# Sums of K through DRAM, a head's product in half the array, and a later transpose of scales in a linear-attention kernel with an FP4 FFN

## The chip, the cores and the metric

One Trainium2 chip, one NeuronCore. The metric is the device time of one execution in microseconds (us). TensorE is called PE here, its weight loads PEld, VectorE DVE, ScalarE ACT, GpSimd POOL and SyncE SP.

## The reference, cut to what matters

The input is 4 batches of 2048 rows of 256 floats. All arithmetic is in fp32.

```python
xn = layernorm(x)
q, k, v = xn @ Wq + bq, xn @ Wk + bk, xn @ Wv + bv      # 16 heads of 64
Q, K = elu(q) + 1, elu(k) + 1
KV = einsum('bshd,bshm->bhdm', K, v)                    # per head 64 x 64
Z  = 1 / (einsum('bshd,bhd->bsh', Q, K.sum(axis=1)) + 1e-6)
o  = einsum('bshd,bhdm,bsh->bshm', Q, KV, Z)
x1 = layernorm(xn + o @ Wo + bo) * g1 + be1
s  = layernorm(x1 + gelu(x1 @ W1 + b1) @ W2 + b2) * g2 + be2
# the gate: inputs and weights of each linear are quantized to FP4 in blocks of 16
h  = silu(fp4_linear(xn, w_gate)) * fp4_linear(xn, w_up)
out = x + s * silu(fp4_linear(h, w_down))
```

## The kernel before

The rows are cut into 32 blocks of 256 (8 per batch, two row tiles of 128 each); block n is worked on in turn n of the main loop. All of a batch's K must be known before its first block, so turn n also computes a part of the next batch's keys: a `sub` is one block of rows with one half (512 columns, 8 heads) of Wk, and two subs go into each turn (16 per batch). Blocks 24 to 31 belong to the last batch and have no subs (`subs` is empty). The first batch's keys and the FP4 quantizing of the weights are done ahead of the loop, in the opening.

**Keys.** V is never formed. Per sub, `keys_k` makes K (tiles pk, k1, e, kk) and adds it to `kacc` on POOL; `keys_xk` adds K^T xn into two PSUM banks, pxk. When a half is complete, `m_of_half` turns it into `m` = (K^T V) Wo. It is a generator and is stepped in three pieces:

1. `pxk` is copied out to `xk` (ACT). `pks`, four products with a column of ones, gives K's sums with the features on the partitions; DVE puts them into `kh`, from which the denominators are made. `pkb`, one product of a matrix of ones with kacc, gives the same sums in a row, the same on all partitions; ACT copies it to `ksum`.
2. `pkv` is K^T xn Wv for four pairs of heads, each as a full 128 x 128 product over two chunks of 128, of which only the two 64 x 64 blocks on the diagonal are used. Eight DVE instructions (L465) add bv times ksum and write these blocks into `kv`, which is zero elsewhere.
3. `pm`, kv times Wo, copied to m.

In the loop the first piece runs at the end of the turns n with n mod 8 = 3 or 7 (n = 3, 7, 11, 15, 19, 23), the other two in the next turn. The first batch's first half is done in the opening, its second half across the opening's end and turn 0.

**The FP4 side.** The products of the gate, pg (gate and up) and pd (down), need their quantized inputs transposed. The grid values (bf16, tile `grid`) are transposed by a DMA into `gridT` (`grid_T`, L549). The block scales (tile `scale`) are small; `spread_scales` transposes them on PE (`pscale`, L533), copies them out on ACT (`scaleT`, L535), stores them to DRAM (`scale_d`, L537), and loads them back with eight DMAs, each of which repeats one row of scales over 16 partitions, into `qT` (L540). `quantized_x` and `quantized_h` then multiply qT by gridT on DVE (L557, L562). In turn n the scales for turn n + 1 are spread: those of h of block n + 1 and of x of block n + 2.

**The order of a turn.** `q_of` (pq, then q1, e, zq), `sums` (pz, the denominators, in four column quarters of the array, then a reciprocal and a broadcast through DRAM), `gate_up` of the next block (pg), `down` (pd), `qz`, `attention` (pa, then the layer norm), the rest of the keys, `ffn_2` of the block before (py), the scales of h and x (L210 to L216), `x1_T` (pt_x, then x1T), `spread_scales`, the last four products of ffn_2, the grid work, `output` of the block before, and `ffn_1` (pf, then hT with Gelu). In a turn without subs, q_of of the next turn follows ffn_1 at once, with pd and pz behind it.

Inside the loop PE keeps the order in which the program writes its instructions (`tc.keep_in_program_order`). The order of the other engines and of the DMA queue on SP comes from a scheduler, which places ready work by its own estimates, so a change in one place can move instructions elsewhere. PSUM has four banks for single products (tag `mm`) and two each for pxk and for running sums (pa, py, pd).

Of the kernel before, what the change touches and what calls it, by code (L numbers as in the profile page):

```python
# [8 lines left out]
F32 = mybir.dt.float32  # L9
BF16 = mybir.dt.bfloat16  # L10
AF = mybir.ActivationFunctionType
ALU = mybir.AluOpType
AX = mybir.AxisListType

P = 128
# [6 lines left out]
def linear_attention_gated_by_fp4_ffn(  # L22
# [34 lines left out]
    nc = tc.nc  # L57
    B, S, D = src.shape
    HD = Wq.shape[1]
    DH = 64  # L60
    FF = W1.shape[1]
    I = w_gate.shape[0]
    ND = D // P
    NH = HD // P
    NF = FF // P
# [12 lines left out]
    work = ctx.enter_context(tc.tile_pool(name="work", bufs=2))  # L78
    small = ctx.enter_context(tc.tile_pool(name="small", bufs=4))
    dram = ctx.enter_context(tc.tile_pool(name="dram", bufs=2 * NB, space=bass.MemoryType.DRAM))  # L80
# [3 lines left out]
    def mm_tile(name):  # L84
        return ps.tile([P, 512], F32, tag="mm", name=name)
# [12 lines left out]
    def mm(*args, **kw):  # L98
        ins = nc.tensor.matmul(*args, **kw)  # L99
        if in_order[0]:  # L100
            tc.keep_in_program_order(ins)
        return ins
# [44 lines left out]
    ones = const.tile([P, P], F32, name="ones")  # L147
# [272 lines left out]
    def m_of_half(b, f, dep=None):  # L420

        nm = f"{b}_{f}"
        fs = slice(f * HALF, (f + 1) * HALF)
        wv = batch.tile([P, ND, HALF], F32, tag="wv", name=f"wv_{nm}", bufs=1)
        load_when(dep, wv, by_chunks(Wv)[:, :, fs])
        wo = batch.tile([P, 4, D], F32, tag="wo", name=f"wo_{nm}", bufs=1)
        load_when(dep, wo, by_chunks(Wo)[:, 4 * f : 4 * f + 4, :])
        if f == 0:
            kh[b] = batch.tile([P, NH, 32], F32, tag="kh", name=f"kh_{b}")
            nc.gpsimd.memset(kh[b], 0.0)  # L430
        m = m_sb[b, f] = batch.tile([P, 4, D], F32, tag="m", name=f"m_{nm}", bufs=3)
        kacc = keys.pop((b, "acc", f))
        pxk = keys.pop((b, "pxk", f))
        xk = batch.tile([P, ND, HALF], F32, tag="xk", name=f"xk_{nm}", bufs=1)
        for d in range(ND):
            nc.scalar.copy(xk[:, d, :], pxk[d])
        pks = mm_tile(f"pks_{nm}")
        for c in range(4):
            mm(
                pks[:, c : c + 1], kacc[:, c * P : (c + 1) * P], ones[:, 0:1],  # L440
                start=True, stop=True,
            )
        for i in range(2):
            hs = slice(i * DH, (i + 1) * DH)
            r0 = 2 * f + i
            nc.vector.tensor_copy(kh[b][hs, 4 * f : 4 * f + 4, r0], pks[hs, :4])
        pkb = mm_tile(f"pkb_{nm}")
        mm(pkb, ones, kacc, start=True, stop=True)
        ksum = work.tile([P, 4, P], F32, tag="e", name=f"ksum_{nm}", bufs=3)
        nc.scalar.copy(ksum, pkb.rearrange("p (c f) -> p c f", c=4))  # L450
        yield
        pkv = mm_tile(f"pkv_{nm}").rearrange("p (c f) -> p c f", c=4)
        kv = work.tile([P, 4, P], F32, tag="kv", name=f"kv_{nm}", bufs=1)
        nc.gpsimd.memset(kv, 0.0)
        for ci in range(4):
            cs = slice(ci * P, (ci + 1) * P)
            for d in range(ND):
                mm(
                    pkv[:, ci, :], wv[:, d, cs], xk[:, d, cs], start=d == 0, stop=d == ND - 1
                )  # L460
        for ci in range(4):
            for h in range(2):
                hs = slice(h * DH, (h + 1) * DH)
                c = 4 * f + ci
                nc.vector.scalar_tensor_tensor(  # L465
                    kv[hs, ci, hs], ksum[hs, ci, hs], cols["bv"][hs, c : c + 1],
                    pkv[hs, ci, hs], ALU.mult, ALU.add,
                )
        yield
        for c2 in range(2):  # L470
            pm = mm_tile(f"pm_{nm}_{c2}").rearrange("p (c d) -> p c d", c=2)
            for ci in range(2):
                mm(
                    pm[:, ci, :], kv[:, 2 * c2 + ci, :], wo[:, 2 * c2 + ci, :],
                    start=True, stop=True,
                )
            nc.scalar.copy(m[:, 2 * c2 : 2 * c2 + 2, :], pm)
        yield
# [221 lines left out]
        nc.gpsimd.tensor_tensor(x1, x1, rows["g1"], ALU.mult)  # L700
        nc.gpsimd.tensor_tensor(x1, x1, rows["shift"], ALU.add)

    def ffn_1(n):
        x1T = blk[n].pop("x1T")
        hT = work.tile([P, NF, T], F32, tag="big", name=f"hT_{n}")
        blk[n]["hT"] = hT
        for cc in range(0, NF, 2):
            pf = mm_tile(f"pf_{n}_{cc}").rearrange("p (c t) -> p c t", c=2)
            for ci in range(2):
                c = cc + ci  # L710
                for d in range(ND):
                    mm(
                        pf[:, ci, :], w1_sb[:, d, c * P : (c + 1) * P], x1T[:, d, :],
                        start=d == 0, stop=d == ND - 1,
                    )
            for ci in range(2):
                c = cc + ci
                nc.scalar.activation(
                    hT[:, c, :], pf[:, ci, :], AF.Gelu, bias=cols["b1"][:, c : c + 1]
                )  # L720

    def ffn_2(n, j, chunks=range(NF)):
        if "py" not in blk[n]:
            blk[n]["py"] = acc_tile(f"py_{n}").rearrange("p (j d) -> p j d", j=TB)
        py, hT = blk[n]["py"], blk[n]["hT"]
        for c in chunks:
            mm(
                py[:, j, :], hT[:, c, j * P : (j + 1) * P], w2_sb[:, c, :],
                start=c == 0, stop=c == NF - 1,
            )  # L730
# [73 lines left out]
    for n in range(NBLK):  # L804
        b, bi = divmod(n, NB)
        subs = (2 * bi, 2 * bi + 1) if b + 1 < B else ()
        if n < last:
            gate = gate_up(n + 1)
        for sub in subs:
            keys_T(b + 1, sub)  # L810
        if subs:
            q_of(n)
            load_xnT(n + 1)
            _, kk_ins = keys_k(b + 1, subs[0])
            with tc.issue_after(kk_ins):
                ins = quantized_x(n)
            with tc.issue_after(sums(n, ins.ins).ins):
                for j in range(TB):
                    quantized_h(n, j)
            step(m_half)  # L820
            keys_xk(b + 1, subs[0])
            step(gate, 9)
            step(m_half)
            down(n, 0)
            down(n, 1)
        elif n < last:
            def values():
                quantized_h(n, 0)
                return quantized_x(n)

            q_of(n, values)
            quantized_h(n, 1)
            load_xnT(n + 1)
            down(n, 0)
            sums(n)
            step(m_half)
            step(gate, 9)
            step(m_half)
            down(n, 1)
        else:  # L840
            for j in range(TB):
                quantized_h(n, j)
                down(n, j)
        with tc.issue_after(blk[n + 1]["late"]) if n < last else nullcontext():
            qz(n)
        if subs:
            keys_k(b + 1, subs[1])
        elif n > 0:
            ffn_2(n - 1, 0, range(NF // 2))
        attention(n)  # L850
        if n + 2 < NBLK:
            load_xn(n + 2)
        if subs:
            keys_xk(b + 1, subs[1])
            if subs[1] % NB == NB - 1:
                m_half = m_of_half(b + 1, subs[1] // NB)
                step(m_half)
        bn, bin_ = divmod(n + 1, NB)
        if bn + 1 < B:
            for sub in (2 * bin_, 2 * bin_ + 1):  # L860
                keys_in(bn + 1, sub)
        if n > 0:
            ffn_2(n - 1, 0, range(0 if subs else NF // 2, NF))
            ffn_2(n - 1, 1, range(NF // 2))
        more = n + 1 < NBLK, n + 2 < NBLK
        if more[0]:
            for j in range(TB):
                scales_h(n + 1, j)
            if more[1]:
                scales_x(n + 2)  # L870
        x1_T(n)
        if more[0]:
            spread_scales(n + 1, *more)
        if n > 0:
            ffn_2(n - 1, 1, range(NF // 2, NF))
        if more[0]:
            grid_of_h(n + 1, 0)
            grid_T(n + 1, 0, NI)
            grid_of_h(n + 1, 1, blk[n]["act"])
            if more[1]:  # L880
                grid_of_x(n + 2, blk[n]["act"])
            grid_T(n + 1, NI, (NCH if more[1] else NI) * TB)
        if n > 0:
            output(n - 1)
        if n + 1 == last:
            q_of(last)
            sums(last)
        ffn_1(n)
    for j in range(TB):
        ffn_2(last, j)  # L890
        output(last, [j])
# [34 lines left out]
```

## Time and profile before

| what | value |
|---|---|
| three runs | 1972.35, 1974.74, 1977.85 us; median 1974.74 |
| profiled execution | 1976.54 us; span of its instructions 1974.8 us |
| mean granted PE clock | 0.996 |
| busy: PE, PEld, DVE, ACT, POOL | 1931.2, 1395.8, 1268.1, 777.1, 536.5 us |
| pkb: products, records | 8, 16; the two start within 0.5 us |
| pkv: products, records, mean ns of one | 64, 128, 275 |
| kv<-ksum,bcol,pkv (DVE, L465) | 64, about 280 ns each |
| ksum copy (ACT, L450) | 8, 588 ns each |
| pscale in the loop and just before | 32, 273 ns each |
| qT<-scale_d, 128 KB each | 248, 5.7 us from issue to landing |
| scale_d<-scaleT, 64 KB | 32, 2.4 us |
| gridT<-grid | 63, 5.4 us |

An fp32 product shows as two records each of weight load (PEld) and matmul (PE). Records overlap, because matmuls are pipelined: the time that a product holds PE is read from the starts, not from its length. A row such as "PE pscale L105 <- DVE scale L215: 9.1, 7, 4.0" says that PE waited for that instruction of DVE 9.1 us in total, 7 times, at most 4.0. "xN" is how many records a row has merged.

### The profile page before, as it was taken

Reading aid. Unit: us, or ns where it says so; the run is one execution under the profiler, and the core shown is the slowest. Engines: PE = TensorE matmul, PEld = TensorE weight load, DVE = VectorE, ACT = ScalarE, POOL = GpSimd, SP = SyncE. Lnnn points to the kernel's source line nnn. Section 1 sums busy time; section 2 is a strip of 40 time slices with the busy share of each in tenths; the row PEclk is TensorE's granted clock in tenths of the full one; section 3 lists DMA queues with packets and bytes.
Section 4 is the critical chain, followed back from the end, with each engine's and each line's share of the span. In section 5 each row is a group of like instructions: output and inputs, shape, how many; then the busy total and the mean of one; then the engine's idle time right before and its main releaser. Section 6 shows DMA issues by size and latency. Waiting matters only on the chain.

```text
span 1974.8 us, 22636 instructions
## 1 busy us (share of the span) xinstructions
PE 1931.2 (98%) x8020; PEld 1395.8 (71%) x8020; DVE 1268.1 (64%) x2319; ACT 777.1 (39%) x1351; POOL 536.5 (27%) x457
## 2 busy tenths in 40 slices
PE   7889999999999999999999999999999999999998
PEld 3445676777776777777777776777766778777777
DVE  7767566656666666666656566665566666677763
ACT  2335433444333444433434423444333443334442
POOL 4332232213233223232223232222232212222221
PEclk9989999999999999999999999999999999999999
DMA  4544433444433544534443534453534434444441
GB/s 148 185 121 87 111 83 92 107 106 80 87 68 82 106 102 91 118 74 108 90 86 61 105 87 85 106 113 65 107 83 81 74 74 81 83 84 80 86 86 41
DMA packets 202104, 183.30 MB, mean 93 GB/s; under 512 B 80236, under 2 KB 161672, under 8 KB 201992
## 3 DMA queue, kind: packets, MB, share of 16 engines
q1 hardware_dynamic: 201576, 181.08, 42.5%
q8 instruction: 63, 1.03, 0.2%
q10 hardware_dynamic: 416, 0.79, 0.1%
q14 instruction: 49, 0.40, 0.1%
HBM read 133.51 MB, written 31.52 MB: 84 GB/s over the span
## 4 chain that ended last, share of the span: by engine, by line
PE 90%; DVE 6%; DMA 2%; ACT 1%; issue 1%; POOL 0%; SPq 0%; POOLq 0%; DVEq 0%; ACTq 0%
PE pg L99 15%; PE pa L99 11%; PE pf L99 11%; PE pq L99 10%; PE pk L99 10%; PE py L99 10%; PE pxk L99 9%; PE pd L99 8%; PE pz L99 2%; DMA gridT<-grid 1%; PE pm L99 1%; PE pt_x L105 1%; PE pkv L99 1%; PE pt_k L105 1%; DVE kk L398 1%
## 5 line engine op out<-in xcount | busy, mean ns | idle before, releaser
L99 PE MATMUL pg<-wgu,qT 128*128 128x352 f32 x1024 | 309.4, 460 | 0.8 <-DVE qT L557 0.8
L99 PEld LDWEIGHTS pg<-wgu,qT 128*128 128x128 f32 x1024 | 193.6, 190 | 118.4 <-issue 12.5
L402 POOL TENSOR_TENSOR kacc<-kacc,kk 128x512 f32<-128x512 f32 x120 | 171.1, 1426 | 337.9 <-DVE kk L398 333.9
L99 PE MATMUL pk<-wk_sb,xnT_k 128*128 128x512 f32 x512 | 238.3, 610 | 4.2 <-ACT xnT_k L371 3.2
L99 PE MATMUL pxk<-kk,xn_k 128*128 128x512 f32 x512 | 233.5, 596 | 1.1 <-DVE kk L398 1.0
L99 PE MATMUL py<-w_sb,hT 128*128 128x256 f32 x1024 | 232.9, 379 | 0.5 <-DVE s L736 0.5
L99 PE MATMUL pf<-x1T,w_sb 128*128 128x256 f32 x1024 | 228.0, 381 | 0.0
L99 PE MATMUL pa<-m,zq 128*128 128x256 f32 x1024 | 227.2, 380 | 0.3 <-ACT g L600 0.3
L99 PE MATMUL pq<-xnT,wq_sb 128*128 128x256 f32 x1024 | 226.3, 379 | 0.0
L99 PEld LDWEIGHTS pa<-m,zq 128*128 128x128 f32 x1024 | 194.0, 190 | 38.7 <-issue 9.8
L99 PEld LDWEIGHTS py<-w_sb,hT 128*128 128x128 f32 x1024 | 192.4, 190 | 35.5 <-issue 11.0
L99 PEld LDWEIGHTS pf<-x1T,w_sb 128*128 128x128 f32 x1024 | 195.6, 191 | 27.3 <-issue 0.4
L99 PEld LDWEIGHTS pq<-xnT,wq_sb 128*128 128x128 f32 x1024 | 193.6, 190 | 25.8
L605 POOL TENSOR_TENSOR o<-g,be_r 128x512 f32<-128x512 f32 x32 | 47.9, 1497 | 504.3 <-ACT g L600 504.3
L99 PEld LDWEIGHTS pk<-wk_sb,xnT_k 128*128 128x128 f32 x512 | 99.7, 197 | 109.3 <-issue 96.3
L637 DVE SCALAR_TENSOR_TENSOR zq<-e,q 128x512 f32<-128x512 f32 x128 | 87.5, 689 | 137.5 <-ACT e L633 137.4
L99 PE MATMUL pd<-wd,qT 128*128 128x256 f32 x768 | 172.2, 379 | 0.1
L693 ACT ACTIVATE x1T<-pt_x,bcol 128x256 f32<-128x256 f32 x64 | 32.8, 563 | 352.7 <-PE pt_x L105 352.7
L99 PEld LDWEIGHTS pxk<-kk,xn_k 128*128 128x128 f32 x512 | 93.4, 190 | 106.8 <-issue 84.2
L99 PEld LDWEIGHTS pd<-wd,qT 128*128 128x128 f32 x768 | 145.8, 190 | 24.1 <-DVE qT L562 0.5
L321 POOL TENSOR_TENSOR rstd<-rstd,neg_half 128x2 f32<-128x2 f32 (+1 forms) x97 | 73.5, 758 | 300.6 <-DVE rstd L320 252.6
L583 ACT ACTIVATE h<-pg 128x352 f32<-128x352 f32 x128 | 59.0, 461 | 212.0 <-PE pg L99 211.9
(129 smaller groups left out, 2453.3 us busy)
## 6 DMA issues: line engine op xcount, KB each, us to landing
zb<-z_d SPq DMA_DIRECT2D x128, 256.0 KB, 6.0
qT<-scale_d SPq DMA_DIRECT2D x248, 128.0 KB, 5.7
x_k<-in_L_attn_src_dram SPq DMA_DIRECT2D x32, 256.0 KB, 2.8
x<-in_L_attn_src_dram SPq DMA_DIRECT2D x32, 256.0 KB, 2.7
xn_d<-xn_k SPq DMA_DIRECT2D x32, 256.0 KB, 2.0
xnT_d<-xnT_k SPq DMA_DIRECT2D x32, 256.0 KB, 5.5
xn<-xn_d SPq DMA_DIRECT2D x32, 256.0 KB, 2.6
xnT<-xnT_d SPq DMA_DIRECT2D x32, 256.0 KB, 2.7
```

The costliest lines, as they stand in the source:

```text
L99: ins = nc.tensor.matmul(*args, **kw)
L105: ins = nc.tensor.transpose(*args, **kw)
L321: nc.gpsimd.tensor_tensor(rstd[:, j0:j1], rstd[:, j0:j1], neg_half[:, j0:j1], ALU.pow)
L398: ins = nc.vector.scalar_tensor_tensor(kk, e, 1.0, k1, ALU.min, ALU.max)
L402: nc.gpsimd.tensor_tensor(kacc, kacc, kk, ALU.add)
L583: nc.scalar.activation(hh, halves[0], AF.Silu)
L605: nc.gpsimd.tensor_tensor(o, g, rows["be2"], ALU.mult)
L637: nc.vector.scalar_tensor_tensor(zq[:, cc : cc + 2, :], e, 1.0, q1, ALU.min, ALU.max)
L693: ins = nc.scalar.activation(x1T[:, c, :], pt[:, c, :], AF.Identity, bias=cols["be1"][:, c : c + 1], scale=cols["g1"][:, c : c + 1],)
```

## The change

It has three parts. First, pkb is dropped: ACT copies the column pks to a small tile `kcol`, SP stores it to DRAM turned round (`k_d`, 4 x 128), and a second DMA loads it into `ksum`, repeated over all partitions. ksum has its own buffer now. Second, pkv is computed per head: sixteen products of 64 columns by 64, the two heads of a pair in the left and right half of the array's columns. Third, `spread_scales` is called later: in turn 0 in the middle of ffn_1, in turns 24 to 30 behind the last four products of ffn_2. In turns 1 to 23 it stays where it was.

```diff
-        pkb = mm_tile(f"pkb_{nm}")
-        mm(pkb, ones, kacc, start=True, stop=True)
-        ksum = work.tile([P, 4, P], F32, tag="e", name=f"ksum_{nm}", bufs=3)
-        nc.scalar.copy(ksum, pkb.rearrange("p (c f) -> p c f", c=4))
+        kcol = small.tile([P, 4], F32, tag="kcol", name=f"kcol_{nm}")
+        nc.scalar.copy(kcol, pks[:, :4])
+        k_d = dram.tile([4, P], F32, tag="k_d", name=f"k_d_{nm}", bufs=2)
+        nc.sync.dma_start(k_d.rearrange("c f -> f c"), kcol)
+        ksum = work.tile([P, 4, P], F32, tag="ksum", name=f"ksum_{nm}", bufs=1)
         yield
-        pkv = mm_tile(f"pkv_{nm}").rearrange("p (c f) -> p c f", c=4)
+        nc.sync.dma_start(
+            ksum, k_d.rearrange("(o c) f -> o c f", o=1).to_broadcast([P, 4, P])
+        )
+        pkv = mm_tile(f"pkv_{nm}")[:, : 4 * DH].rearrange("p (c f) -> p c f", c=4)
...
         for ci in range(4):
-            cs = slice(ci * P, (ci + 1) * P)
             for d in range(ND):
-                mm(
-                    pkv[:, ci, :], wv[:, d, cs], xk[:, d, cs], start=d == 0, stop=d == ND - 1
-                )
+                for h in range(2):
+                    cs = slice(ci * P + h * DH, ci * P + (h + 1) * DH)
+                    mm(
+                        pkv[h * DH : (h + 1) * DH, ci, :], wv[:, d, cs], xk[:, d, cs],
+                        start=d == 0, stop=d == ND - 1,
+                    )
...
-                    pkv[hs, ci, hs], ALU.mult, ALU.add,
+                    pkv[hs, ci, :], ALU.mult, ALU.add,
...
-    def ffn_1(n):
+    def ffn_1(n, half_way=None):
...
         for cc in range(0, NF, 2):
+            if half_way is not None and cc == NF // 2:
+                half_way()
...
         x1_T(n)
-        if more[0]:
+        if subs and n > 0:
             spread_scales(n + 1, *more)
         if n > 0:
             ffn_2(n - 1, 1, range(NF // 2, NF))
+        if more[0] and not subs:
+            spread_scales(n + 1, *more)
...
-        ffn_1(n)
+        ffn_1(n, None if n else lambda: spread_scales(1, True, True))
```

## The prediction

> **What bounds the kernel now.** I read the page first: the slices, then the chain that ended last.
>
> ```profile
> PE   7889999999999999999999999999999999999998
> DVE  7767566656666666666656566665566666677763
> PE 90%; DVE 6%; DMA 2%; ACT 1%; issue 1%; POOL 0%; SPq 0%; POOLq 0%; DVEq 0%; ACTq 0%
> ```
>
> PE (TensorE) is full from the third slice on, 90% of the chain is PE, and DVE has a third of its time free. So a microsecond of PE work taken out of the main loop is a microsecond of time, unless PE then meets a wait that its work had covered; and a wait of PE in the main loop costs its full length. PE's waits, next, are few. One row belongs to the transpose that is moved:
>
> ```profile
> PE pscale L105 <- DVE scale L215: 9.1, 7, 4.0
> ```
>
> By its tile's instructions these are block 0 (4.0 us) and the blocks 24 to 29, which have no keys to compute: three waits of 0.3 us and three of 1.44 us. Block 30 and the blocks with keys have none. Then PE's timeline at a batch boundary (columns: start, length, engine, line, operation):
>
> ```profile
> 1584.69 0.95 PE L99 MATMUL pks<-ones,kacc 128*128 128x1 f32 x8
> 1585.50 1.10 PE L99 MATMUL pkb<-kacc,ones 128*128 128x512 f32 x2
> 1586.44 5.34 PE L99 MATMUL py<-w_sb,hT 128*128 128x256 f32 x24
> ...
> 1610.40 1.45 PE L99 MATMUL pz<-zq,kh 128*32 128x256 f32 x16
> 1611.77 2.05 PE L99 MATMUL pkv<-xk,wv 128*128 128x128 f32 x16
> 1613.66 9.63 PE L99 MATMUL pg<-wgu,qT 128*128 128x352 f32 x32
> ```
>
> Read it by starts, since lengths overlap: pkb holds PE from 1585.50 to 1586.44, 0.94 us; pkv from 1611.77 to 1613.66, 1.89 us (a product is two records, 0.112 us apart in pkv). Nothing waits between them.
>
> **What the skill says.** (1) The Trainium skill, "TensorEngine Tiling (Array Packing)", Key Properties: column tiles work independently, and a change of tiling mode drains the array. The trace agrees: pz already uses quarters (128*32), and in short windows of its timeline four records start together at 1610.40, the next four at 1610.64, then 1610.85, so four products of 256 columns take about 0.215 us, one product's time; from pz's last group, started at 1611.46, to pkv is 0.31 us, so the change of mode costs about 0.1 us beyond the 0.21 us of work. (2) "TensorE: Matmul & The Clock Gate", Part 1: an idle window of some 3.4 us halves PE's clock. The trace agrees at block 0:
>
> ```profile
> 221.00:226.00 5.00, 0.78 (x4) 0.45 (x4) 4.48 (x11) 1.70 (x3) 3.35 (x4) 1.00 0.03 10
> 226.00:230.00 4.00, 3.96 (x12) 3.18 (x13) 3.14 (x6) 2.18 (x4) 1.55 (x2) 0.58 0.73 241
> ```
>
> The first figure is the stretch, then each engine's busy time; PEclk is third from the end. After 4 us of idle PE the clock is 0.58, and the FFN's first product there (pf, 32 records) takes 8.6 us from start to the next tile instead of 6.9. (3) The same page, on queue depths: ScalarE and VectorE are strict first-in, first-out. The tail below rests on it. (4) "DMA: Bandwidth & Descriptors", Rules for kernel authors: a strided last dimension is one descriptor per element. The new k_d store, 128 partitions by 4 floats turned round, is 512 elements of 4 bytes; no DMA of before is like it.
>
> **The change, part by part, on PE's path.**
>
> *Row sums through DRAM.* pkb goes: 0.94 us at each of the six boundaries inside the loop (blocks 3, 7, 11, 15, 19, 23), **5.6 us**. ACT gets a 128x4 copy for one of 588 ns; that is off the path. SP gets two issues per half, which in the built order stand, in the loop, right before the scale store or the loads of the next keys; the second waits for the first to land. Behind it queue the scale store and its eight broadcasts. In block 23 the copy can be done near 1586, the scale store is due at about 1592.5 (1593.5 now, less 0.94), so the landing may take some 5 us before SP delays it; scale_d lands in 2.4 us and xn_d in 2.0 us, and 512 small elements I put at 3 (2 to 8). The broadcast of 256 KB is like xn_d's loads, 2.6 us, and DVE needs it only 20 us later. Cost taken: 0, to 1 us above.
>
> *K^T xn Wv in halves.* 8 products of 128x128 become 16 of 64x64. If two run together as four do in pz, and loads hide there as in pz, 32 records are 16 pairs of about 0.056 us (half of pkv's 0.112): 0.9 us. Entering costs a weight load less than now; leaving for pg adds a mode change and an exposed load, 0.1 + 0.1. So 1.2 us for 1.89: 0.7 each, six in the loop, **4.3 us**. Bounds: 0.9 each with no switch cost; if the halves run one after the other, 32 x 0.056 + 0.2 = 2.0, a loss of 0.1.
>
> *First batch, f=1 (before and in block 0).* PE would reach pg 1.6 us sooner, but pg waits for DVE's qx (0.84 us now), and that for the gridT transpose; the eight kv instructions (2.3 us) move behind it. I take **0.6**, 0 to 1.6.
>
> *First batch, f=0 (the opening, near 88 to 110 us).* PE waits for DVE's weight quantizing there (2.3 us at 91.87, 1.7 at 108.18), so savings go into these waits. New: ksum's load stands on SP behind five row loads (last issue 99.86) and lands near 103.5 to 104 where DVE wants it at 102.5; behind it wait wgu and wd on DVE; k_d also holds up a wgu load by 1 us. **-0.5**, +1 to -3.
>
> *Block 0's transpose in the middle of ffn_1.* pf can start when x1T is there (ACT, 222.09 + 1.02), so PE works from 222.7 through half of pf to 226.2; the scale (DVE, done 225.9) is ready. But on ACT the second hT now stands behind m_x, which waits for y (228.9), so pf's last chunk finds its PSUM buffer only at 230.0 and pf ends at 231.7, against 234.8 now (which has the wait and the slow clock). **3.0 us**, 1 to 5. The broadcasts start some 4 us later; here qx is 22 us away, so they stay hidden.
>
> *Blocks 24 to 29: transpose behind four products of ffn_2.* PE fills its wait: 3 x 0.3 + 3 x 1.44 = 5.2 us. But look at what follows it (ACT, then DVE, block 25):
>
> ```profile
> 1685.37 1.02 ACT L693 ACTIVATE x1T<-pt_x,bcol 128x256 f32<-128x256 f32 x2 [12.37 <-PE pt_x L105]
> 1687.14 0.27 ACT L535 COPY scaleT<-pscale 128x128 f32<-128x128 f32 x1 [0.74 <-PE pscale L105]
> 1687.30 0.80 ACT L235 ACTIVATE m_h<-h 128x704 bf16<-128x704 f32 x1
> 1688.67 0.63 ACT L235 ACTIVATE m_x<-y 128x512 bf16<-128x512 f32 x1 [0.57 <-DVE y L231]
> ...
> 1701.26 0.96 DVE L562 TENSOR_TENSOR qT<-qT,gridT 128x768 f32<-128x768 f32 x1 [4.81 <-DMA qT<-scale_d]
> ```
>
> The built order puts scaleT behind m_x on ACT, and m_x waits for DVE's y. So scaleT starts near 1689.2 instead of 1687.14, 2.05 us later (1.56 in the blocks with the short wait). With it go scale_d, eight broadcasts and, on SP behind them, gridT; DVE already waits for them (4.81 us), multiplies, and only then makes the zq that pz needs. Measured from pscale, in the three blocks where qx starts late (15.36, 15.49, 15.93) pg starts 4.57 after it; the other three (13.8 to 14.1) have pg at its floor, 19.39. Adding the shift: typical blocks get 15.3 + 4.6 = 19.9 (short wait) or 16.0 + 4.6 = 20.6 (long); two in six have a slow store, 1.6 more, as now. Sum 3 x 19.9 + 3 x 20.55 + 3.2 = 124.6 against 118.7 now: **-5.9 us** net, since both are in DVE's time, which the change leaves; the 5.2 are given back within each block. Bounds: +5 if all hides, -12 if stores are slow in all.
>
> *Block 30.* No wait to win; its eight broadcasts now stand behind gridT on SP, some 3.5 us later; its products are due 3.8 us after they are made. 0.
>
> Sum: 5.6 + 4.3 + 0.6 - 0.5 + 3.0 - 5.9 = 7.1 us. The profiled execution took 1976.54 (span 1974.8), inside the range of the three runs; taken off the median, 1974.74: **1967.6 us**.
>
> **Rivals.**
> 1. *The scale chain is hidden in the tail after all*: the 5.2 us stay won in place of 5.9 lost, 18.2 in all: 1956.5. For: the six blocks wait for nothing but the scale at pscale. Against: the 4.81 us above. Chance 0.15.
> 2. *The change doesn't do what it says: halves run one after the other.* Then pkv costs 2.0 and 4.9 us go: 1972.5. Against: pz's four together. Chance 0.17.
> 3. *Slower: the late scales in the tail.* The same mechanism in full: if the store of the scales is slow in every block (3.0 us to the first broadcast in block 25, 1.6 in block 24) and the waits for pd grow to 3.5 us, so that the clock halves as in block 0. It decides from a tail loss of 13.0 + 5.9 = 19 us, 3.2 a block. At 3.5 a block: 21 us lost, 1982.7. Chance 0.12.
>
> The forecast has 0.52, the rest 0.04.
>
> **From cases to numbers.** 0.3%, 5.9 us, is about what a measurement of this kernel can tell from no change. The forecast's own range is 1963 to 1973, some six tenths of it beyond 5.9 us. With rival 1, faster is 0.53; with rival 2 and the forecast's weak end, same 0.33; slower 0.14. The range reaches down to rival 1 and up past rival 2 to its bounds, and leaves out rival 3 and a part of the rest: 1956.5 to 1977.5.
>
> **What would show it.** Right: pkb gone and pks followed by py at once; pkv near 1.2 us in pairs; PEclk 1.0 at block 0; PE's wait for DVE scale gone; scaleT behind m_x in blocks 24 to 29, and new waits of PE at pd or pz on qT. Wrong: pg still 19.4 us after the scale is ready; pkv at 2 us; SP's k_d landing over 5 us; PE waits in the opening grown by more than 3 us.

## The result, and the profile after

| | before | after |
|---|---|---|
| median of 4 runs each | 1974.83 us | 1984.32 us |
| lowest to highest | 1972.35 to 1977.85 | 1982.2 to 1986.56 |
| profiled execution; span | 1976.54; 1974.8 | 1982.2; 1980.3 |

The ratio is 1.0048, 95% interval 1.003 to 1.0065: the change makes the kernel 9.5 us **slower**. The forecast was 1967.6, with a range up to 1977.5: it is wrong, and on the other side. The profiled execution of after is the lowest of its four runs and that of before lies 1.7 us above its median, so the profiles show 5.5 us of the 9.5.

The page of after, its slices and its chain:

```profile
PE   7878999999999999999999999999999989999998
PE 83%; DVE 7%; DMA 6%; issue 1%; SPq 1%; ACT 1%; POOL 1%; DVEq 0%; POOLq 0%; ACTq 0%
```

PE's work has shrunk (1921.8 us busy, 1931.2 before), yet its share of the chain falls from 90% to 83%, while DMA goes from 2% to 6%. Three slices are a digit lower: the third (the opening), the fourth, which ends with block 0's wait, and the thirty-third, from 1584 us on, where the last batch's boundary (block 23) is. The waits of PE name them (waiting tile, releaser: total, times, longest):

```profile
PE pd L99 <- DVE qT L570: 9.8, 7, 5.8
PE pg L99 <- DVE qT L565: 7.2, 1, 7.2
PE pxk L99 <- DVE kk L398: 5.1, 4, 3.7
...
PE pwgu L105 <- issue: 3.0, 1, 3.0
```

The row "pscale <- DVE scale" (9.1 us) is gone as meant. In its place PE waits 7.2 us once for pg, in block 0, and 5.8 once for pd, at block 23; the other six waits at pd, 4.0 together, are in the tail. The 3.7 and 3.0 are in the opening. What they share is in the DMA rows (out<-in, queue, count, size, median from issue to landing) and in SP's waits:

```profile
k_d<-kcol SPq DMA_DIRECT2D x8, 2.0 KB, 10.4
ksum<-k_d SPq DMA_DIRECT2D x8, 256.0 KB, 4.2
```

```profile
SPq L454 <- DMA k_d<-kcol: 51.2, 7, 10.6
```

The store of 2 KB takes 10.4 us to land, over twice the 256 KB load behind it, and SP stands still for it. (The trace has a landing for two of the eight stores, 11.5 us in the opening and 9.3 at block 23. At the other boundaries of the loop ksum's load, which waits for it, is issued 8.7 to 11.6 us after it.) The boundary at block 23, PE's timeline of after:

```profile
1583.37 0.95 PE L99 MATMUL pks<-ones,kacc 128*128 128x1 f32 x8
1584.18 5.43 PE L99 MATMUL py<-w_sb,hT 128*128 128x256 f32 x24
...
1611.54 4.53 PE L99 MATMUL pd<-wd,qT 128*128 128x256 f32 x12 [5.84 <-DVE qT L570]
1616.00 1.07 PE L99 MATMUL pz<-zq,kh 128*32 128x256 f32 x16
1617.01 1.15 PE L99 MATMUL pkv<-xk,wv 128*64 128x64 f32 x32
1618.09 6.18 PE L99 MATMUL pg<-wgu,qT 128*128 128x352 f32 x20
```

pks runs straight into py: pkb is gone. pkv, 32 records in half columns, holds PE from 1617.01 to 1618.09, 1.08 us for the 1.89 of before. But pd ahead of it waited 5.84 us, and then took 4.46 us from its start to pz instead of 2.69 (1607.71 to 1610.40 before). SP's queue in the same stretch, after:

```profile
1584.97 0.37 SPq L451 DMA_DIRECT2D k_d<-kcol  x1
1594.32 0.32 SPq L454 DMA_DIRECT2D ksum<-k_d  x1
1594.73 0.39 SPq L545 DMA_DIRECT2D scale_d<-scaleT  x1
1599.47 3.63 SPq L548 DMA_DIRECT2D qT<-scale_d  x8
```

and before:

```profile
1593.47 0.32 SPq L537 DMA_DIRECT2D scale_d<-scaleT  x1
1595.06 3.63 SPq L540 DMA_DIRECT2D qT<-scale_d  x8
```

Count from pscale (1589.88 after, 1592.06 before). The scale store is issued 4.85 us later instead of 1.41: 3.44 us are SP's wait for k_d. From that store to the first broadcast it takes 4.74 us instead of 1.59: 3.15 more, with SP waiting for nothing but the landing of the scale store. DVE's first multiplication into qT starts 20.65 us after pscale, before 13.91, so it is 6.7 us late; the two delays make 6.6 of it. They are not of one kind: the trace shows the first as a wait for k_d, but when the scale store goes out k_d has landed (1594.30), and the load of ksum, 256 KB, stands 0.41 us ahead of it.

Block 0, two stretches of after (columns: stretch, then busy time of PE, PEld, DVE, ACT, POOL; PEclk third from the end):

```profile
189.00:196.00 7.00, 0.36 (x1) 0.00 (x0) 0.22 (x1) 0.00 (x0) 0.00 (x0) 0.69 1.22 179
196.00:200.00 4.00, 3.48 (x6) 2.19 (x7) 3.97 (x5) 0.46 (x1) 0.00 (x0) 0.50 0.95 271
231.00:238.00 7.00, 5.58 (x25) 4.46 (x25) 6.33 (x12) 3.54 (x6) 3.50 (x4) 1.00 0.41 119
```

In the first row nearly every engine stands still for 7 us while DMAs run, and the granted clock falls to 0.50: pg's 32 records take 12.36 us, 9.73 before. In turn 0's ffn_1 (the last row) the clock is 1.00 where it was 0.58, as forecast. The Trainium skill, "TensorE: Matmul & The Clock Gate", Part 1 (idle halves the clock), holds here with these numbers; the change has moved that cost from one place to another.

### The profile page after: what moved, and what is told of

Read it like the earlier page. It is cut to its first block, busy times and chain, and to the rows that moved or that the text cites. A ratio compares the mean times of both kernels' runs of the same rounds, so it can differ in the third digit from the quotient of the medians.

```text
span 1980.3 us, 22889 instructions
## 1 busy us (share of the span) xinstructions
PE 1921.8 (97%) x8132; PEld 1385.3 (70%) x8132; DVE 1266.9 (64%) x2319; ACT 771.9 (39%) x1351; POOL 534.9 (27%) x457
## 4 chain that ended last, share of the span: by engine, by line
PE 83%; DVE 7%; DMA 6%; issue 1%; SPq 1%; ACT 1%; POOL 1%; DVEq 0%; POOLq 0%; ACTq 0%
PE pg L99 15%; PE pa L99 11%; PE pk L99 10%; PE pxk L99 9%; PE py L99 9%; PE pf L99 8%; PE pq L99 8%; PE pd L99 8%; DMA qT<-scale_d 2%; PE pz L99 2%; DMA gridT<-grid 1%; DMA wgu<-in_L_ffn_w_up_dram 1%; PE pm L99 1%; DVE kk L398 1%; PE pt_k L105 1%
## 5 line engine op out<-in xcount | busy, mean ns | idle before, releaser
L99 PE MATMUL pk<-wk_sb,xnT_k 128*128 128x512 f32 x512 | 233.4, 599 | 5.1 <-ACT xnT_k L371 4.0
L99 PEld LDWEIGHTS pk<-wk_sb,xnT_k 128*128 128x128 f32 x512 | 97.7, 192 | 107.4 <-issue 93.8
```

## Where the time went, stretch by stretch

The spans of all profiles, cut at the same six instructions (starts in PE's timeline): the opening's pscale, block 0's pg, the pscale of turn 1, that of turn 23, the pg behind it, and the end of the span. Us in each stretch:

| kernel | opening | to pg of block 0 | turn 0 | turns 1 to 23 | boundary 23 | tail | span |
|---|---|---|---|---|---|---|---|
| before | 124.6 | 65.9 | 94.1 | 1307.4 | 21.6 | 361.1 | 1974.8 |
| after | 127.4 | 69.1 | 93.8 | 1299.5 | 28.2 | 362.2 | 1980.3 |
| E1 after, pkb back | 123.9 | 63.3 | 91.2 | 1305.0 | 20.6 | 363.9 | 1967.9 |
| E2 DRAM sums alone | 127.8 | 69.6 | 96.9 | 1302.3 | 29.0 | 356.5 | 1982.1 |
| E3 halves alone | 121.5 | 63.3 | 94.7 | 1305.0 | 20.8 | 357.4 | 1962.8 |
| E5 after, rows stored | 127.2 | 64.9 | 92.5 | 1300.2 | 20.4 | 366.1 | 1971.3 |
| E7 later tail alone | 123.4 | 65.8 | 94.5 | 1307.4 | 21.7 | 364.2 | 1977.1 |
| E8 after, ksum by POOL | 127.5 | 71.6 | 94.1 | 1299.5 | 27.4 | 365.1 | 1985.2 |
| E9 halves + turn 0 | 121.2 | 63.3 | 91.2 | 1305.0 | 21.0 | 357.6 | 1959.3 |
| E10 E9 + rows in the loop | 121.3 | 63.3 | 91.2 | 1300.2 | 20.4 | 358.8 | 1955.2 |
| E11 unread stores | 123.8 | 64.3 | 94.6 | 1307.4 | 24.2 | 358.3 | 1972.7 |
| E12 E10 + later tail, scaleT first | 123.5 | 63.3 | 91.2 | 1300.2 | 20.4 | 359.0 | 1957.6 |
| E13 unread stores, small | 124.3 | 64.6 | 94.1 | 1307.4 | 21.6 | 357.1 | 1969.1 |

The opening scatters by 2 to 3 us between kernels that do the same there (E1, E3, E9, E10, E12: 121.2 to 123.9), the tail by 4 to 5; the stretches between are steadier. Against before, after wins 7.9 us in turns 1 to 23 and loses 6.6 at boundary 23, 3.2 up to block 0's pg, 2.8 in the opening and 1.1 in the tail. Turn 0 shows only 0.3 won because pg at half clock eats what the later transpose gains.

## The experiments

**Theory**: the row sums' way through DRAM loses what the rest wins, by the late landing of k_d. Within it, (A) it is only SP that waits, or (B) the store, while it is in flight, also delays the transfers issued behind it. **Rival**: the late scales in the tail, or the halves, do it.

**E1: after, with pkb back.**

```diff
-        kcol, k_d, store, load
+        mm(pkb, ones, kacc, start=True, stop=True)
+        nc.scalar.copy(ksum, pkb.rearrange("p (c f) -> p c f", c=4))
```

> The changed kernel with pkb and its ACT copy back in place of the DRAM round trip; halves and later transposes stay. Theory (the 512-element store lands in about 10 us and holds up SP and what shares its rings): PE's waits of 5.8 us at pd in block 23, 7.2 us at pg in block 0 and the new 3 to 4 us waits near 100 to 112 us go, pkb's 0.94 us comes back six times; about 1984.3 - 16 - 2 (slow clock in block 0) - 3 + 5.6 = 1969. Rival (the later transposes or the halves are what costs, or the scheduler's other order in the opening): stays at 1980 or above.

Measured 1971.35 us, ratio to before 0.9985 (0.9977 to 0.9994). The waits at pg and at boundary 23 are gone; what remains at pd is the tail's:

```profile
PE pd L99 <- DVE qT L565: 4.5, 6, 2.0
```

Undoing this one part is worth 13 us: the rest of the change is a gain of 2.8.

**E2: before, with only the sums through DRAM.**

> The kernel before with the DRAM round trip alone. Theory: six times 0.94 us won (5.6), opening, block 0 and block 23 lose about 3, 8 and 6: 1975 + 11 = 1986, k_d landing in 9 to 12 us as in the changed kernel. Rival (the other two parts cost): at or below 1975.

1984.68 us, ratio 1.0055 (1.0043 to 1.0067), with PE's waits of 7.0 us at pg and 5.4 at boundary 23. This part alone is a loss of 10.5 us, and the halves and the tail are not needed for it. Theory and rival are told apart here.

**E3: before, with only the halves.**

```diff
-        mm(pkv[:, ci, :], wv[:, d, cs], xk[:, d, cs], ...)
+        for h in range(2):                       # cs: 64 columns of head h
+            mm(pkv[h*DH:(h+1)*DH, ci, :], wv[:, d, cs], xk[:, d, cs], ...)
```

> The kernel before with pkv in halves of the array alone. Theory (in the changed kernel's trace pkv went from 1.89 to 1.08 us): 0.8 us each at the six boundaries of the loop, the first batch's two go into waits: 1974.2 - 4.9 = 1969. Rival (halves bring nothing once the mode changes are paid): 1974.

1964.69 us against 1973.44, ratio 0.9961 (0.9947 to 0.9975): 8.7 us, more than expected. The two profiles are 12.0 us apart: 2.4 in turns 1 to 23, 0.8 at boundary 23, 3.1 in the opening and 2.6 from there to block 0's pg; turn 0 is 0.6 longer. The remaining 3.7 are in the tail, where both kernels do the same, and are scatter.

**E7: before, with only the later transpose in the tail.**

```diff
-        if more[0]:
+        if subs:
             spread_scales(n + 1, *more)
...
+        if more[0] and not subs:                 # behind the last products of ffn_2
+            spread_scales(n + 1, *more)
```

> The kernel before with the later transpose in turns 24 to 30 alone. Theory (scaleT behind m_x, qT later, pd and pz wait): by the traces so far, from turn 24's pg to the end the moved kernels take 315 to 319 us, the unmoved 310 and 315: a loss of 1 to 6 us, 1978. Rival (PE's waits of 0.3 and 1.4 us at pscale stay won): 1969 to 1972.

1977.84 us, ratio 1.0026 (1.0016 to 1.0035): a loss of 4.4 us in medians. So the late scales in the tail do lose time, as the theory of this run had it, but far less than the 10.5 us of E2; as a rival to k_d they are too small to decide.

**E5: after, with PE turning kcol (128 x 4) into 4 rows first, so that k_d is stored as 4 pieces of 512 bytes.**

```diff
+        tr(pkr, kcol, ident)
+        nc.scalar.copy(krow, pkr)
-        nc.sync.dma_start(k_d.rearrange("c f -> f c"), kcol)
+        nc.sync.dma_start(k_d, krow)
```

`m_of_half` gets one more step for it: the transpose and the store come later in the turn than the copy into kcol, just ahead of `x1_T`.

> The changed kernel with one edit: PE transposes kcol once more (128x4 to 4x128, about 0.1 us, later in the turn), so that the store to DRAM is 4 rows of 512 bytes and no longer 512 elements of 4 bytes; the bytes and the load of ksum are the same. Theory (it is the number of elements): k_d lands in 1.5 to 2.5 us, the waits at block 23, block 0 and most of the opening's go: 1964 to 1969. Rival (a DRAM round trip on SP costs whatever its shape, or other parts cost): within 3 us of 1984.

1973.14 us, ratio 0.9991 (0.9983 to 1.0). In the loop it does what was expected: boundary 23 takes 20.4 us, and ksum can be issued 1.8 us after k_d. It missed the expected time by 4 us. The table puts most of that ahead of the loop: the opening is as long as that of after, where the load of ksum is late whatever the store does. DVE's timeline of E5:

```profile
107.54 2.34 DVE L478 SCALAR_TENSOR_TENSOR kv<-ksum,bcol,pkv 64x64 f32<-64x64 f32 x8 [4.83 <-DMA ksum<-k_d]
```

ksum is issued at 100.42, right behind five row loads and not held up by the store, and DVE has it 7 us later. wgu's turn on DVE comes only then, and PE has a gap of 7.2 us at its transpose pwgu. So in the opening the round trip costs time by its load too, not by the store alone.

**E8: after, with ksum's load issued by POOL.** SP no longer waits for k_d.

```diff
-        nc.sync.dma_start(
+        nc.gpsimd.dma_start(
             ksum, k_d.rearrange("(o c) f -> o c f", o=1).to_broadcast([P, 4, P])
```

> The changed kernel with one edit: the load of ksum, which waits for the store's landing, is issued from POOL instead of SP. Theory A (SP's wait in program order is what delays the scales): scale_d in block 23 is issued near 1.4 us after pscale, PE's 5.8 us wait there goes, the opening and block 0 keep theirs: about 1978. Theory B (the store's elements fill the rings, and what is issued behind it lands late in any case): scale_d is issued early and lands late, and the time stays within 2 us of 1984.

1986.93 us, ratio 1.0064 (1.0049 to 1.0079). SP's queue at boundary 23, where pscale is at 1592.75:

```profile
1587.84 0.37 SPq L451 DMA_DIRECT2D k_d<-kcol  x1
1594.15 0.32 SPq L545 DMA_DIRECT2D scale_d<-scaleT  x1
1599.73 4.02 SPq L548 DMA_DIRECT2D qT<-scale_d  x8
```

The scale store now goes out on time, 1.40 us after pscale; but the broadcasts start 5.58 us behind it, where 1.59 were enough before. (A) alone falls: with SP's wait away the stretch still takes 27.4 us. ksum's load is issued at 1598.98 here (POOL), when 4.83 of the 5.58 us have passed, so it can hardly be what holds up the scale store; whether it delays the broadcasts themselves is not told apart in this run.

**E11: before, with unread stores of kcol turned round at the loop's boundaries: 128 elements in batch 1, 256 in batch 2, 512 in batch 3.** No load, no wait.

```diff
+        nc.scalar.copy(kcol, pks[:, :4])
+        nc.sync.dma_start(k_d[:w].rearrange("c f -> f c"), kcol[:, :w])   # w = 1, 2, 4
```

> The kernel before, with only a scaled copy of ksum's columns on ACT (kcol) and a store of part of it to DRAM that nothing reads: 1 column (128 elements of 4 bytes) in batch 1, 2 columns (256) in batch 2, 4 columns (512) in batch 3, at the six boundaries of the loop. No load of sums, no wait of SP for the landing, TensorE's and VectorE's work as before. Theory A (only SP's wait for the landing costs): no PE wait at block 23, time as before within 2 us, about 1974 to 1976. Theory B (the store's elements occupy the DMA rings, and what is issued behind them lands late): landing grows with the number of elements, about 3, 5.5 and 10 us; scale_d and the broadcasts of qT behind 512 elements land 3 to 5 us late, a PE wait of 3 to 5 us at block 23's pd that is not there before, time about 1978.

1976.88 us against 1975.03, ratio 1.0015 (1.0008 to 1.0022). SP's queue at boundary 23:

```profile
1584.40 0.37 SPq L456 DMA_DIRECT2D k_d4x<-kcol  x1
1591.57 0.32 SPq L543 DMA_DIRECT2D scale_d<-scaleT  x1
1596.19 3.63 SPq L546 DMA_DIRECT2D qT<-scale_d  x8
```

A store that nobody waits for or reads, issued 7.2 us earlier, puts the scale store's broadcasts 4.62 us behind it instead of 1.59, and PE waits 1.7 us there; the stretch takes 24.2 us, 21.6 before. That is (B), 3.0 us of lateness, with the slow store still in flight for 1.6 us when the scale store goes out (it lands at 1593.13). The 3.15 us in after are of the same size, but not the same case: there SP has waited, k_d has landed, and ksum's load stands ahead. Whether that load or an after-effect of the store makes them is not shown; no run issues ksum's load ahead of the scale store without the slow store. The half of the expectation on sizes failed: the landings known, one each, are 7.2 us for 128 elements, 10.3 for 256 and 8.7 for 512. The first broadcast of qT is 0.9 and 4.5 us later than in before at the two boundaries with 128, 2.4 and 4.7 with 256, 3.2 and 3.0 with 512. Neither grows steadily with the number.

**E13: the same with other sizes: 8 and 32 elements of 4 bytes, and the 128 x 4 tile as it stands, 128 pieces of 16 bytes.**

> As the store that nothing reads, with other sizes: 8 elements of 4 bytes (one column of 8 partitions) in batch 1, 32 elements in batch 2, and in batch 3 the 128 x 4 tile as it stands, 128 pieces of 16 bytes; otherwise the kernel before. If it is the number of pieces that makes the store slow, 8 and 32 pieces leave the first broadcast of qT within 1 us of where the kernel before has it at the same block, and 128 pieces of 16 bytes delay it at block 23 by 1 us or less (a quarter of 512). If any store of small pieces by this route delays what follows, the first broadcast is 2 us or more late in all, at block 23 about 3 us as behind 512 pieces, and PE waits there about 1.7 us. Time between that of before and 3 us above.

One execution, 1971.11 us (before in the same comparison, one as well, 1974.98), so only its trace is used. The DMA rows:

```profile
k_d32y<-kcol SPq DMA_DIRECT2D x2, 0.1 KB, 5.1
k_dw<-kcol SPq DMA_DIRECT2D x2, 2.0 KB, 1.9
```

The same 2 KB, not turned round, land in 1.9 us; the first broadcast at boundary 23 is where the kernel before has it (2.98 us after pscale, 3.00), and the stretch takes 21.6 us. 128 pieces of 4 bytes took 7.2 us in E11, so at an equal count it is the piece of 4 bytes that is slow (one landing each, at different boundaries). With 8 and 32 elements the broadcasts come within 0.7 us of before, though 32 elements still take 5.1 us to land. Why pieces of 4 bytes are so slow is not shown.

**E9: halves, and the later transpose in turn 0 only.**

> pkb kept, pkv in halves, the later transpose in turn 0 only (turns 24 to 30 as before). Theory (halves win 5, turn 0 wins 3 to 5, the tail's move loses): 1974.2 - 5 - 4 = 1965, below the kernel that has pkb back and all later transposes (1971). Rival (the tail's move wins): 1972 or more.

1962.61 us, ratio 0.9945 (0.9933 to 0.9958). Turn 0 takes 91.2 us for E3's 94.7: the step is worth 3.5 us in the profiles, 2.1 in the medians.

**E10: E9 with the rows' store of E5 in batches 1 to 3, pkb kept for the first.**

> The same, and the batches 1 to 3 get their row sums by a store of four 512-byte rows (one more PE transpose of 0.1 us) instead of pkb; the first batch keeps pkb, since in the opening DVE waited 4.8 us for ksum's load behind the row loads. Theory: 0.94 - 0.15 us more at six boundaries, 4.7 us below the same kernel with pkb: 1960. Rival (any DRAM round trip on SP at the boundary costs what pkb did): the same as with pkb.

**1957.46 us**, ratio 0.9918 (0.9905 to 0.9932): 16 us below the kernel before of the same comparison (1973.44), and 5.1 below E9. This version is faster than before and after. Its boundary at block 23, SP's queue:

```profile
1576.03 0.28 SPq L462 DMA_DIRECT2D k_d<-krow  x1
1577.39 0.34 SPq L557 DMA_DIRECT2D scale_d<-scaleT  x1
1577.82 0.37 SPq L466 DMA_DIRECT2D ksum<-k_d  x1
1578.99 3.65 SPq L560 DMA_DIRECT2D qT<-scale_d  x8
```

The store has landed by 1577.82, and the broadcasts start 1.60 us behind the scale store, as before.

**E12: E10 with the later transpose in the tail too, but with m_x behind scaleT on ACT.**

```diff
+            behind = spread_scales(n + 1, *more)  # returns ACT's copy into scaleT
...
+                grid_of_x(n + 2, behind)          # m_x follows it
```

> e10 (pkb back for the first batch, K^T xn Wv in halves, the later transpose in turn 0, sums through rows of 512 bytes in the other batches; 1957.5 us) plus the later transpose of the scales in turns 24 to 29, but with ACT's copy of m_x issued behind scaleT instead of ahead of it. Theory (in the tail it is ACT's order, m_x ahead of scaleT, that made the later transpose lose): scaleT ends within 0.3 us of the transpose, no PE wait at pd in the tail above 0.5 us, and 1953 to 1958 us. Rival (the transpose itself is too late for the broadcasts there, whatever ACT's order): the pd waits of 0.3 to 1.7 us stay and the time is 1960 to 1963.

1958.69 us, ratio 0.9915 (0.9902 to 0.9929), not told apart from E10. The ACT order, and what waits for it, block 25 of after (ACT, then DVE):

```profile
1692.35 0.63 ACT L235 ACTIVATE m_x<-y 128x512 bf16<-128x512 f32 x1 [0.29 <-DVE y L231]
1692.89 0.25 ACT L543 COPY scaleT<-pscale 128x128 f32<-128x128 f32 x1
...
1705.62 0.96 DVE L570 TENSOR_TENSOR qT<-qT,gridT 128x768 f32<-128x768 f32 x1 [4.40 <-DMA qT<-scale_d]
```

and of E12 (pscale at 1672.05):

```profile
1672.36 0.27 ACT L555 COPY scaleT<-pscale 128x128 f32<-128x128 f32 x1
1672.53 0.63 ACT L235 ACTIVATE m_x<-y 128x512 bf16<-128x512 f32 x1
```

scaleT comes 0.31 us after pscale, in after 1.00 (pscale at 1691.89). Over all profiles the tail takes 364.3 us on the mean where the transpose is late (after, E1, E5, E7, E8: 362.2 to 366.1) and 358.1 where it is early (before, E2, E3, E9, E10, E11, E13: 356.5 to 361.1). With scaleT first it takes 359.0. A narrower stretch says the same: from the start of pt_x to pg the six blocks 24 to 29 take 126.1 us together where the transpose is early (124.6 to 128.6), 132.0 where it is late (129.7 to 134.2), and 126.9 in E12. So ACT's order explains some 5 of the 6 us that the later transpose loses. The hoped gain did not come: PE's 4 us of waits for the scale in E10 are gone, but it now waits 1.3 us at pd in block 26 and 0.9 in block 28, where none above 0.5 was expected, and the tail is no shorter.

## Why the prediction was wrong, by its steps

**The failed step: "512 small elements I put at 3 (2 to 8)", and "Cost taken: 0, to 1 us above".** The landing is 10.4 us, above the upper bound. The bound came from scale_d (2.4 us) and xn_d (2.0), whose pieces are not of 4 bytes. The step had cited the Trainium skill, "DMA: Bandwidth & Descriptors", Rules for kernel authors (one descriptor per element of a strided last dimension), and the trace agrees: after moves 4352 more packets under 512 bytes than before, and 8 x 512 = 4096 would be these elements. But it had priced them like fewer and larger ones. Beyond the size, a mechanism was left out in the loop: the step asked only when SP is held up, not what a store in flight does to the transfers behind it (E8, E11). For the opening the prediction did let k_d hold up a wgu load, by 1 us; for the store ahead of block 0's pg it priced nothing. The cost, from the table, with the kernels that have the halves and the first batch's pkb (boundary 23: E1) as the measure:

- opening: 127.4, against 122.3 on the mean of E1, E3, E9, E10, E12: 5 us lost, forecast -0.5 with +1 to -3. k_d goes out at 91.57, half a us ahead of the wgu load, and DVE then waits 7.0 us for that. E5 shows that the load of ksum would cost it as well.
- up to block 0's pg: 69.1 against 63.3, 5.8 us, forecast as a gain of 0.6. k_d is issued at 173.17, between scale_d and its eight broadcasts, whose issue then takes 11.54 us for 3.75. Then pg at half clock, 2.6 us.
- boundary 23: 28.2 against 20.6 (E1), 7.6 us, forecast 0. About half of the lateness is SP's wait for k_d, 3.44 us, and the other half, 3.15, is the scale store's slow landing behind ksum's load, whose cause is open (E11). The wait at pd of 5.84 us also costs 1.8 by the clock, which is 0.60 from 1611 to 1616.
- boundaries 3 to 19: nothing, though scale_d is 4 to 8 us after pscale there. In before DVE's first multiplication into qT comes 24.6 to 25.5 us after pscale there, at block 23 13.9. The same delay is free at five places and costs 7.6 us at the sixth.

With the 2.6 us of the slow pg that is 21 us lost, against the 5.5 that pkb's removal wins (1305.0 to 1299.5), 15.5 net; E1 and after are 13 us apart, since E1's own opening was 1.6 slower than that mean and its tail 1.7 slower than after's.

**pkb gone, 5.6**: 4.8 (E9 to E10, which adds a small transpose on PE) to 5.5 (E1 to after) measured. Right.

**Halves, 4.3 in the loop**: 3.2 (2.4 + 0.8). The size at the place was nearly right, 0.81 us each for 0.7, and the two halves do run side by side: pkv's records start in pairs, the two of a pair within 0.01 us, a pair every 0.058 us. So rival 2 falls. But where pxk follows pkv, 0.27 us comes back: from pxk's start to pg it takes 3.60 us instead of 3.44, and pg 9.57 instead of 9.46. Why is open.

**First batch**: the halves win some 2 us up to block 0's pg (63.3 in all kernels with halves and pkb there, 64.3 to 65.9 without halves) and perhaps 1.7 in the opening (mean of before, E7, E11, E13 124.0, to 122.3), which is within the scatter there. The forecast let most of these savings vanish in waits. In after, k_d takes both.

**Turn 0's transpose, 3.0**: 3.5 in the profiles, 2.1 in the medians. The predicted wait for ACT is there as well, 1.8 us at pf.

**The tail, -5.9**: -6.2 on the means of the whole tail, -5.9 from pt_x to pg, -4.4 in E7's medians, and by the order on ACT that the prediction named (E12). The delay has the size forecast too: scaleT starts 3.3 or 4.7 us after pt_x's start instead of 1.7 or 2.6, where 1.6 to 2.1 later was forecast. Rival 1 falls; rival 3's mechanism is there, but nowhere near the 3.2 us a block from which it would decide. So without k_d's cost the sum of 7.1 us would have been about right: E1's gain of 2.8 and pkb's 5.5, which E1 lacks, make 8.3.

The slower outcome came from a case that was not among the rivals: a store of 2 KB. The prediction listed its landing over 5 us among the signs of being wrong, but gave it neither a cost nor a chance. Two of its sums are off, without bearing on the outcome: six times 0.7 us make 4.2, and six tenths of 0.52 with rival 1's 0.15 make 0.46 for faster where it has 0.53. And in the pz that it read for the pairing only the first eight records start in fours; the other eight start two at a time.

## What to carry to other kernels

Here the same 2 KB landed in some 10 us or in 2, by the size of the pieces. So price a small transfer by its pieces and not by its bytes: search the profile for a transfer with the same piece, and where there is none let the upper bound be generous and ask too what is issued behind it. A latency put in at a place that the program runs eight times has to be held against the slack at each of the eight; here it was free at five, and the other three decided. A PE instruction of 0.94 us can be the cheapest way to spread a value over partitions; turning 128 x 4 into rows by PE first made the way through DRAM pay.

## What the runs showed of the hardware

- A store from SBUF to DRAM in pieces of 4 bytes lands late: 512 elements in 8.7 to 11.5 us (after, E2, E8, E11), 256 in 10.3, 128 in 7.2 (E11), 32 in 5.1 (E13), the last three one landing each. 128 pieces of 16 bytes took 1.9 (E13), 4 rows of 512 bytes at most 2.0 at the loop's boundaries (E5, E10).
- A transfer issued on the same queue 7 us later, while the slow store is in flight, still feels it: scale store to first broadcast 4.62 us for 1.59 (E11), with no instruction waiting for the slow store.
- fp32 products of 64 columns by 64 run side by side in two halves of the array: 32 records in 1.08 us, for 16 full ones in 1.89.
- After 7 us without work PE's clock is 0.50, and 32 records of pg take 12.36 us instead of 9.73.
